# Layer 0 of a two-layer metaformer: where the scan's VectorE instructions wait for the other engines

## The chip, the cores and the metric

The kernel runs on one core of a Trainium2 chip. The metric is the device time of one launch in microseconds (us). A profile is one further execution, recorded by the hardware profiler; its own time stands beside its span below.

## The reference

Two layers, each a token mixer and a small feed-forward network with residuals, over an image of 2 x 96 channels x 96 x 96. Only the mixer of layer 0 is touched. It projects to 192 inner channels, bends the image by a learnt offset, and runs a selective scan over windows of 6 x 6 tokens in four directions (`kg` = 0 to 3), with 16 states for every inner channel:

```python
def step(hst, inputs):
    ut, dt, bt, ct = inputs
    dA = jnp.exp(dt[..., None] * A)
    hst = hst * dA + (dt * ut)[..., None] * bt[:, :, None, :]
    y = jnp.einsum('bkdn,bkn->bkd', hst, ct)
    return (hst, y)
h0 = jnp.zeros((Bt, K_, Dd, N), u.dtype)
_, ys = jax.lax.scan(step, h0, (us, ds, bs, cs))
return jnp.moveaxis(ys, 0, -1) + Dv[None, :, :, None] * u
```

## The kernel before

Layer 0 takes the two images in 32 stripes of 6 image rows (576 tokens, 16 windows). A stripe has three parts: `_l0_front` (norm, projection, convolution, offsets, sampling, the step sizes and B and C of the scan), `_l0_scan` and `_l0_back` (norm, gate, projection, feed-forward).

`_l0_scan` runs, for a stripe, over two halves of the channels (`h`), two token orders (`o`) and two directions (`kk`): eight sections. A section (`_l0_section`) has four quarters (`i`) of four states each, and a quarter has two units (`c` = 0 and 1, 288 tokens each). That is 1024 quarters and 2048 units in all. Counting the units through the whole layer, unit u and unit u+1 with u even make a quarter. Partitions hold 32 channels x 4 states; three channel blocks lie along the free axis, so an operation of a unit has 128 x 864 elements.

A quarter begins with a DMA of C (`cre`) and three ScalarE exponentials (line 997) that make the decays `dA` of both its units, in one of two buffers. A unit is then, in order of the data:

- **B** (line 1008): a TensorE matmul spreads a row of B over the partitions, into one of two PSUM buffers `B`.
- **product** (line 1011): VectorE multiplies it by `dur` (step size times input) into the single PSUM buffer `bp`.
- **scan** (line 1021): VectorE's scan of `dA` and `bp` into one of six buffers `h` (`P.nh` = 6).
- **times C** (line 1024): GpSimd multiplies `h` by `cre` in place.
- **states** (line 1034): TensorE sums over the states into the accumulator `y`.

So a product waits for its B, and for the scan before it, which reads the one buffer `bp`. A scan waits for its product, for its decays, and for the buffer `h` that the unit six before it used: that unit's times C and states. The scan of unit u+1 takes the buffer of unit u-5.

The order on each engine is written out by a planner: `_Plan.op` records every operation with a cost, the tiles that it reads and writes, and a due time; `_Plan.order` plays the engines forward and sorts all operations by planned start; `_Plan.issue` emits them in that order, and `_in_order` holds each engine to it. Semaphore waits are put in afterwards, where an instruction needs a later tick of another engine than its own engine has already waited for.

Of the kernel before, what the change touches and what calls it, by code (L numbers as in the profile page):

```python
# [12 lines left out]
AF = mybir.ActivationFunctionType  # L13
ALU = mybir.AluOpType
# [18 lines left out]
H2 = T // 2  # L33
# [4 lines left out]
NBL = C // CB  # L38
# [17 lines left out]
def _in_order(k, tc, start, engines=ENGINES):  # L56

    last = {}
    for i in k.nc.cur_bb.bb.instructions[start:]:
        if i.engine in engines:  # L60
            if i.engine in last:
                tc.add_manual_dep(
                    i,
                    last[i.engine].name,
                    mybir.DependencyInfo(
                        mybir.DependencyClass.NoSync, mybir.DependencyReason.DATA
                    ),
                    reason="in_order",
                )
            last[i.engine] = i  # L70
# [865 lines left out]
def _l0_scan(k, P, S, n, f, tau):  # L936


    nc = k.nc
    f.Y = S.tile(P.hand, [C, 2, T], "Y", 1)  # L940
    for h in range(2):

        py = S.tile(P.ps, [128, 512], "y", 1)
        t0 = (64 * n + 32 * h) * tau

        def direct(h=h, py=py):

            for b in range(NBL):
                w = k.w_D[:, h, b * CB : b * CB + CB]
                v = f.xs0.ap[:, h]  # L950
                nc.tensor.matmul(py.ap[b * CB : b * CB + CB, :HEAD], w, v[:, :HEAD],
                                 start=True, stop=False)
                nc.tensor.matmul(_tail(py, b), w, v[:, HEAD:], start=b == 0, stop=False)

        S.op("pe", 1.4, direct, (f.xs0,), (py,), due=t0)
        for o in range(2):
            for kk in range(2):
                _l0_section(k, P, S, f, o, h, kk, py, t0 + (16 * o + 8 * kk) * tau, tau)

        def out(h=h, py=py):  # L960
            nc.scalar.copy(f.Y.ap[:, h, :HEAD], py.ap[:C, :HEAD])
            for b in range(NBL):
                nc.scalar.copy(f.Y.ap[b * CB : b * CB + CB, h, HEAD:], _tail(py, b))

        S.op("act", 1.4, out, (py,), (f.Y,), due=t0 + 33 * tau)
# [5 lines left out]
def _tail(py, b):  # L971

    n = T - HEAD
    return py.ap[NBL * CB :, b * n : b * n + n]


def _l0_section(k, P, S, f, o, h, kk, py, at, tau):
    nc = k.nc
    kg = o + 2 * kk
    reps = []  # L980
    for name, d in (("dlr", f.dl[kg]), ("dur", f.du[kg])):
        t = S.tile(P.rep, [128, NBL, T], name, 2)
        S.op("sp", 2.6, lambda t=t, d=d: nc.sync.dma_start(
            t.ap.rearrange("p b t -> p (b t)"),
            d.ap[:, 3 * h : 3 * h + 3, :].rearrange("c b t -> c (b t)").unsqueeze(1)
            .to_broadcast([CB, NQ, NBL * T])), (d,), (t,), due=at - 9 * tau)
        reps.append(t)
    dlr, dur = reps

    def quarter(i):  # L990
        t0 = at + 2 * i * tau
        cre, dA = S.tile(P.rep, [128, T], "cre", 4), S.tile(P.rep, [128, 2, NBL, H2], "dA", P.nda)
        S.op("sp", 1.0, lambda: nc.sync.dma_start(
            cre.ap, f.cd[o].ap[kk, :, i, :].unsqueeze(0).to_broadcast([CB, NQ, T])),
            (f.cd[o],), (cre,), due=t0 - P.early["sp"] * tau)
        for blk in range(NBL):
            S.op("act", 0.76, lambda blk=blk: nc.scalar.activation(  # L997
                dA.ap[:, :, blk, :], dlr.ap[:, blk, :].rearrange("p (c n) -> p c n", c=2),
                AF.Exp, scale=k.A[:, i, kg, h, blk : blk + 1]),
                (dlr,), ((dA, blk),), due=t0 - P.early["act"] * tau, tab="e")  # L1000
        for c in range(2):
            unit(i, c, cre, dA, t0 + c * tau)

    def unit(i, c, cre, dA, t0):
        toks = slice(c * H2, (c + 1) * H2)
        pB, bp = S.tile(P.ps, [128, 512], "B", 2), S.tile(P.ps, [128, 1024], "bp", 1)
        ht = S.tile(P.rep, [128, NBL, H2], "h", P.nh)
        S.op("pe", 0.3, lambda: nc.tensor.matmul(  # L1008
            pB.ap[:, :H2], k.selb[:, kk, i, :], f.bc[o].ap[:, toks], start=True, stop=True),
            (f.bc[o],), (pB,), due=t0 - P.early["pe"] * tau)  # L1010
        S.op("dve", 1.13, lambda: nc.vector.tensor_tensor(  # L1011
            bp.ap[:, : NBL * H2].rearrange("p (b n) -> p b n", b=NBL), dur.ap[:, :, toks],
            pB.ap[:, :H2].unsqueeze(1).to_broadcast([128, NBL, H2]), ALU.mult),
            (dur, pB), (bp,), due=t0 - P.early["dve"] * tau)

        def scan():
            hv, dv = (v.rearrange("p b n -> p (b n)") for v in (ht.ap, dA.ap[:, c]))
            bv = bp.ap[:, : NBL * H2]
            if kk:
                hv, dv, bv = hv[:, ::-1], dv[:, ::-1], bv[:, ::-1]  # L1020
            nc.vector.tensor_tensor_scan(hv, dv, bv, 0.0, ALU.mult, ALU.add)  # L1021

        S.op("dve", 2.0, scan, (dA, bp), (ht,), due=t0 + (1.35 - P.early["dve"]) * tau)
        S.op("pool", 2.06, lambda: nc.gpsimd.tensor_tensor(  # L1024
            ht.ap, ht.ap, cre.ap[:, toks].unsqueeze(1).to_broadcast([128, NBL, H2]), ALU.mult),
            (cre,), (ht,), due=t0 + (2.3 - P.early["pool"]) * tau)

        def states():
            end = o == 1 and kk == 1 and i == NQ - 1

            def part(dst, v, stop):
                if o:
                    v = v.rearrange("p (w j i) -> p w i j", i=WIN, j=WIN)
                nc.tensor.matmul(dst, k.fold, v, start=False, stop=stop)  # L1034

            for blk in range(NBL):
                dst = py.ap[CB * blk : CB * blk + CB]
                n = HEAD - H2 if c else H2
                part(dst[:, c * H2 : c * H2 + n], ht.ap[:, blk, :n], end and c == 1)
            if c:  # L1040
                for blk in range(NBL):
                    part(_tail(py, blk), ht.ap[:, blk, n:], end and blk == NBL - 1)

        S.op("pe", 1.0, states, (ht,), (py,), due=t0 + (3.5 - P.early["pe"]) * tau)

    for i in range(NQ):
        quarter(i)


def _layer0(k, tc, a, x, x2d):  # L1050


    nc = k.nc
    with ExitStack() as st:
        P = Ctx()
        pool = lambda name, bufs, **kw: st.enter_context(tc.tile_pool(name=name, bufs=bufs, **kw))
        cp = pool("l0c", 1)
        P.dram = pool("scr", 1, space=DRAM)
        with ExitStack() as ws:
            tmp = ws.enter_context(tc.tile_pool(name="l0t", bufs=1))  # L1060
            wps = ws.enter_context(tc.tile_pool(name="l0p", bufs=1, space=PSUM))
            _l0_weights(k, a, cp, tmp, wps, P.dram)
            ffn = _ffn_weights(k, cp, tmp, "f0", a["W1_0"], a["b1_0"], a["W2_0"], a["b2_0"])
        P.front, P.hand, P.rep, P.back = (pool(n, 1) for n in ("front", "hand", "rep", "back"))
        P.ps = pool("ps0", 1, space=PSUM)
        P.early = {"pe": 60, "act": 60, "dve": -30, "pool": 0, "sp": 8}
        P.np, P.ng, P.nda, P.nh = 3, 5, 2, 6
        start = len(nc.cur_bb.bb.instructions)
        S, tau = _Plan(k), 3.4
        stripes = [(b, s) for b in range(NB) for s in range(NW)]  # L1070
        F = [Ctx() for _ in stripes]

        def front(n):
            if n < len(stripes):
                t0, t1 = (64 * n - 90) * tau, (64 * n - 12) * tau
                _l0_front(k, P, S, F[n], x, *stripes[n], lambda v: t0 + v * (t1 - t0))

        def back(n):
            b, s = stripes[n]
            t0, t1 = (64 * n + 68) * tau, (64 * n + 135) * tau  # L1080
            _l0_back(k, P, S, F[n], ffn, x[b, :, s * WIN : (s + 1) * WIN, :],
                     x2d[b, :, s * T : (s + 1) * T], lambda v: t0 + v * (t1 - t0))

        front(0)
        for n in range(len(stripes)):
            front(n + 1)
            _l0_scan(k, P, S, n, F[n], tau)
            back(n)
        S.issue()
        _in_order(k, tc, start, ENGINES + (mybir.EngineType.SP,))  # L1090
# [760 lines left out]
```

## Time and profile before

| | us |
|---|---|
| median of 3 runs (9014.46 to 9014.84) | 9014.57 |
| profiled execution, its own time | 9021.88 |
| span of its trace, first to last instruction | 9020.1 |
| first product starts (layer 0's scans begin) | 172.4 |
| last scan starts | 6887.6 |
| VectorE busy in the whole span | 8098.6 (90%) |

Between 172.4 and 6887.6 us the layer's fronts, scans and backs overlap stripe by stripe; what follows is layer 1. In the profile, DVE is VectorE, ACT ScalarE, POOL GpSimd, PE TensorE, PEld TensorE's weight load, and L1021 is line 1021. An instruction of type EVENT_SEMAPHORE carries nothing but waits; the engine's sequencer runs it, and it is not counted as busy. A gap of the engine under 150 ns is not put down to a releaser by the profile: it is shown only in the idle sums.

### The profile page before, as it was taken

Reading aid. Unit: us, or ns where it says so; the run is one execution under the profiler, and the core shown is the slowest. Engines: PE = TensorE matmul, PEld = TensorE weight load, DVE = VectorE, ACT = ScalarE, POOL = GpSimd, SP = SyncE. Lnnn points to the kernel's source line nnn. Section 1 sums busy time; section 2 is a strip of 40 time slices with the busy share of each in tenths; the row PEclk is TensorE's granted clock in tenths of the full one; section 3 lists DMA queues with packets and bytes.
Section 4 is the critical chain, followed back from the end, with each engine's and each line's share of the span. In section 5 each row is a group of like instructions: output and inputs, shape, how many; then the busy total and the mean of one; then the engine's idle time right before and its main releaser. Section 6 shows DMA issues by size and latency. Waiting matters only on the chain.

```text
span 9020.1 us, 122080 instructions
## 1 busy us (share of the span) xinstructions
PE 7473.2 (83%) x43537; PEld 3552.9 (39%) x43537; DVE 8098.6 (90%) x5663; ACT 6393.2 (71%) x10720; POOL 6194.7 (69%) x3931
## 2 busy tenths in 40 slices
PE   6888788888878887888788888878866999989998
PEld 3343334444434443344344444334423333543345
DVE  2999999999999999999999999999996898969988
ACT  4677777777777777777777777777754777677867
POOL 3988888888888888888888888898874000320013
PEclk9889888988888888888898989888866999999999
DMA  2444444444444444444444444444442000010000
GB/s 75 138 140 142 140 139 145 140 141 141 135 140 139 135 147 140 141 142 139 144 140 137 142 136 141 137 140 139 138 140 68 3 3 4 21 30 2 3 9 24
DMA packets 335679, 969.58 MB, mean 107 GB/s; under 512 B 50424, under 2 KB 52144, under 8 KB 334768
## 3 DMA queue, kind: packets, MB, share of 16 engines
q1 hardware_dynamic: 335056, 961.64, 33.7%
q8 instruction: 346, 5.67, 0.3%
q14 instruction: 277, 2.27, 0.1%
HBM read 788.04 MB, written 132.17 MB: 102 GB/s over the span
## 4 chain that ended last, share of the span: by engine, by line
DVE 39%; PE 14%; issue 3%; ACT 2%; POOL 1%; DVEq 1%; DMA 0%; SPq 0%; POOLq 0%; ACTq 0%
DVE h L1021 19%; DVE bp L1011 11%; DVE sums L1426 6%; PE sc L1352 4%; DVE acc L1585 3%; PE av L1413 3%; PE y L1034 1%; PE pp L1601 1%; PE pd L669 0%; PE nxc L1113 0%; POOL e L1550 0%; DVEq L1021 0%; PE pk L1125 0%; PE px L608 0%; PE pv L1157 0%
## 5 line engine op out<-in xcount | busy, mean ns | idle before, releaser
L1024 POOL TENSOR_TENSOR h<-h,cre 128x864 f32<-128x864 f32 x2048 | 4122.8, 2021 | 826.7 <-DVE h L1021 415.0
L1021 DVE TENSOR_TENSOR_SCAN h<-dA,bp 128x864 f32<-128x864 f32 x2048 | 4001.5, 1954 | 252.3 <-PE y L1034 6.4
L997 ACT ACTIVATE dA<-dlr,A 128x576 f32<-128x576 f32 x3072 | 2157.0, 765 | 1219.5 <-DVE h L1021 1127.9
L1011 DVE TENSOR_TENSOR bp<-dur,B 128x864 f32<-128x864 f32 x2048 | 2175.8, 1062 | 257.2 <-DMA dur<-du_d 45.5
L1034 PE MATMUL y<-h,fold 128*32 128x288 f32 (+2 forms) x18432 | 1877.9, 454 | 106.3 <-POOL h L1024 102.2
L1008 PE MATMUL B<-bt,selb 128*128 128x288 bf16 x2048 | 637.6, 313 | 1095.3 <-DVE bp L1011 1087.5
L536 PE MATMUL pc<-xin,off 96*96 96x288 f32 x4608 | 1325.0, 414 | 0.9 <-ACT xin L501 0.9
L1034 PEld LDWEIGHTS y<-h,fold 128*32 128x32 f32 x18432 | 766.0, 119 | 1359.0 <-issue 623.2
L1356 ACT ACTIVATE pr<-sc 128x960 f32<-128x960 f32 (+1 forms) x1080 | 955.4, 937 | 258.0 <-DVE sums L1426 146.1
L1426 DVE TENSOR_TENSOR sums<-sums,pr 128x1920 f32<-128x1920 f32 (+1 forms) x510 | 1059.2, 2077 | 60.2 <-ACT pr L1356 7.0
L536 PEld LDWEIGHTS pc<-xin,off 96*96 96x96 f32 x4608 | 708.0, 164 | 622.8 <-issue 379.9
L1507 POOL MEMSET vch<- 96x32 f32 x16 | 2.0, 125 | 1312.8 <-DVE dist L1385 1269.0
L1352 PE MATMUL sc<-qH,kH 32*128 32x480 f32 (+1 forms) x3240 | 710.2, 602 | 9.8 <-DMA q<-qH 9.8
L1352 PE MATMUL sc<-q,kH 32*128 32x480 f32 (+1 forms) x1080 | 564.3, 602 | 0.0
L1413 PE MATMUL av<-pr,vT 128*32 128x480 f32 (+1 forms) x4320 | 532.9, 564 | 3.8 <-ACT av L1430 3.5
L1585 DVE SCALAR_TENSOR_TENSOR acc<-vch,lepe_w,acc 96x1152 f32<-96x1152 f32 x304 | 489.9, 1612 | 7.6
L1008 PEld LDWEIGHTS <-selb 128*128 128x128 bf16 x2048 | 201.9, 100 | 710.5 <-issue 634.5
L1352 PEld LDWEIGHTS sc<-qH,kH 32*128 32x128 f32 x3240 | 285.0, 184 | 439.6 <-issue 304.3
L709 PE MATMUL pt<-xd,w_dt 96*128 96x288 f32 x768 | 317.5, 506 | 25.9 <-ACT zs L519 13.9
L728 POOL TENSOR_TENSOR e<-e,du 128x576 f32<-128x576 f32 x192 | 271.0, 1412 | 32.2 <-ACT du L724 32.0
L1550 POOL TENSOR_TENSOR e<-e,mask 100x384 f32<-100x384 f32 x96 | 171.5, 1808 | 175.6 <-ACT e L1548 175.3
L730 POOL TENSOR_TENSOR dl<-dl,r 128x576 f32<-128x576 f32 x192 | 270.2, 1407 | 6.2
(260 smaller groups left out, 10182.2 us busy)
## 6 DMA issues: line engine op xcount, KB each, us to landing
cre<-c_d SPq DMA_DIRECT2D x1024, 288.0 KB
dur<-du_d SPq DMA_DIRECT2D x256, 864.0 KB
dlr<-dl_d SPq DMA_DIRECT2D x256, 864.0 KB
x<-xs SPq DMA_DIRECT2D x512, 72.0 KB
du_d<-du SPq DMA_DIRECT2D x128, 288.0 KB
dl_d<-dl SPq DMA_DIRECT2D x128, 288.0 KB
du_d<-du SPq DMA_DIRECT2D x128, 144.0 KB
dl_d<-dl SPq DMA_DIRECT2D x128, 144.0 KB
```

Source lines behind the costliest of these rows:

```text
L536: pe(H2, lambda: nc.tensor.matmul(pc.ap[:C, :H2], k.w_c1[:, ih, tap, oh * C : (oh + 1) * C], xin.ap[:, ih, 3 * c + dy : 3 * c + dy + 3, dx ...
L997: S.op("act", 0.76, lambda blk=blk: nc.scalar.activation(dA.ap[:, :, blk, :], dlr.ap[:, blk, :].rearrange("p (c n) -> p c n", c=2), AF.Exp ...
L1008: S.op("pe", 0.3, lambda: nc.tensor.matmul(pB.ap[:, :H2], k.selb[:, kk, i, :], f.bc[o].ap[:, toks], start=True, stop=True), (f.bc[o],), (p ...
L1011: S.op("dve", 1.13, lambda: nc.vector.tensor_tensor(bp.ap[:, : NBL * H2].rearrange("p (b n) -> p b n", b=NBL), dur.ap[:, :, toks], pB.ap[: ...
L1021: nc.vector.tensor_tensor_scan(hv, dv, bv, 0.0, ALU.mult, ALU.add)
L1024: S.op("pool", 2.06, lambda: nc.gpsimd.tensor_tensor(ht.ap, ht.ap, cre.ap[:, toks].unsqueeze(1).to_broadcast([128, NBL, H2]), ALU.mult), ( ...
L1034: nc.tensor.matmul(dst, k.fold, v, start=False, stop=stop)
L1352: nc.tensor.matmul(two[s // 2][:, s % 2, :n], kH[rows, k0 : k0 + 128], q, start=True, stop=True)
L1356: nc.scalar.activation(pr[:, 2 * i : 2 * i + 2, :n], two[i][:, :, :n], AF.Exp, scale=HD**-0.5)
L1413: nc.tensor.matmul((main if s < HEADS else other)[s * HD : (s + 1) * HD, :n], vT[:, blk, hd, :], pr[:, s, :n], start=at == 0, stop=at == e ...
L1426: nc.vector.tensor_tensor(sums[:, :, :n], sums[:, :, :n], pr[:, :, :n], ALU.add)
L1585: S.op("dve", 1.6, lambda: nc.vector.scalar_tensor_tensor(acc.ap, src(), W.lw[:, t : t + 1], acc.ap, ALU.mult, ALU.add), (vch,), (acc,))
```

## The change

The first product of each quarter (`c` = 0) is given extra dependencies, as semaphore waits: on the last exponential of its quarter, on the B matmul of the unit after it, and on the times C and the last states matmul of unit u-5, whose `h` the quarter's second scan reuses. They are looked up in `P.issued`, a dictionary that is filled as instructions are emitted; what has not been emitted by then is left out. Nothing is said to the other three VectorE instructions of the quarter, which need the same ticks or earlier ones. No operation is added or removed, and costs, tiles and due times given to the planner are the same. `first` is the first unit of the stripe's half, 64 n + 32 h. The last line of the diff stands at the end of `states`.

```diff
-def _l0_section(k, P, S, f, o, h, kk, py, at, tau):
+def _l0_section(k, P, S, f, first, o, h, kk, py, at, tau):
     nc = k.nc
+    latest = lambda: nc.cur_bb.bb.instructions[-1]
+    def wait(keys):
+        for other in map(P.issued.get, keys):
+            if other is not None:
+                P.tc.add_manual_dep(
+                    latest(), other.name,
+                    mybir.DependencyInfo(mybir.DependencyClass.Sync, mybir.DependencyReason.DATA),
+                    reason="with_the_product")
...
-        t0 = at + 2 * i * tau
+        t0, u = at + 2 * i * tau, first + 16 * o + 8 * kk + 2 * i
...
+            def decay(blk=blk):
+                nc.scalar.activation(...)
+                P.issued["act", u] = latest()
...
+        def spread():
+            nc.tensor.matmul(...)
+            P.issued["B", u] = latest()
+
+        def product():
+            nc.vector.tensor_tensor(...)
+            if c == 0:
+                free = u + 1 - P.nh
+                wait([("act", u), ("B", u + 1), ("pool", free), ("pe", free)])
...
+        def times_c():
+            nc.gpsimd.tensor_tensor(...)
+            P.issued["pool", u] = latest()
...
+            P.issued["pe", u] = latest()
```

More of the change, by code (lines that the diff above doesn't have):

```diff
@@ L957, in _l0_scan @@
             for kk in range(2):
-                _l0_section(k, P, S, f, o, h, kk, py, t0 + (16 * o + 8 * kk) * tau, tau)
+                _l0_section(k, P, S, f, 64 * n + 32 * h, o, h, kk, py, t0 + (16 * o + 8 * kk) * tau, tau)
         def out(h=h, py=py):
@@ L996, in quarter, with unit @@
         for blk in range(NBL):
[L997 to L1000, printed above, removed]
+            def decay(blk=blk):
+                nc.scalar.activation(
+                    dA.ap[:, :, blk, :], dlr.ap[:, blk, :].rearrange("p (c n) -> p c n", c=2),
+                    AF.Exp, scale=k.A[:, i, kg, h, blk : blk + 1])
+                P.issued["act", u] = latest()
+            S.op("act", 0.76, decay, (dlr,), ((dA, blk),), due=t0 - P.early["act"] * tau, tab="e")
         for c in range(2):
-            unit(i, c, cre, dA, t0 + c * tau)
-    def unit(i, c, cre, dA, t0):
+            unit(u + c, i, c, cre, dA, t0 + c * tau)
+    def unit(u, i, c, cre, dA, t0):
         toks = slice(c * H2, (c + 1) * H2)
@@ L1007, in unit @@
         ht = S.tile(P.rep, [128, NBL, H2], "h", P.nh)
[L1008 to L1014, printed above, removed]
+        def spread():
+            nc.tensor.matmul(
+                pB.ap[:, :H2], k.selb[:, kk, i, :], f.bc[o].ap[:, toks], start=True, stop=True)
+            P.issued["B", u] = latest()
+        def product():
+            nc.vector.tensor_tensor(
+                bp.ap[:, : NBL * H2].rearrange("p (b n) -> p b n", b=NBL), dur.ap[:, :, toks],
+                pB.ap[:, :H2].unsqueeze(1).to_broadcast([128, NBL, H2]), ALU.mult)
+            if c == 0:
+                free = u + 1 - P.nh
+                wait([("act", u), ("B", u + 1), ("pool", free), ("pe", free)])
+        S.op("pe", 0.3, spread, (f.bc[o],), (pB,), due=t0 - P.early["pe"] * tau)
+        S.op("dve", 1.13, product, (dur, pB), (bp,), due=t0 - P.early["dve"] * tau)
         def scan():
@@ L1023, in unit @@
         S.op("dve", 2.0, scan, (dA, bp), (ht,), due=t0 + (1.35 - P.early["dve"]) * tau)
-        S.op("pool", 2.06, lambda: nc.gpsimd.tensor_tensor(
-            ht.ap, ht.ap, cre.ap[:, toks].unsqueeze(1).to_broadcast([128, NBL, H2]), ALU.mult),
-            (cre,), (ht,), due=t0 + (2.3 - P.early["pool"]) * tau)
+        def times_c():
+            nc.gpsimd.tensor_tensor(
+                ht.ap, ht.ap, cre.ap[:, toks].unsqueeze(1).to_broadcast([128, NBL, H2]), ALU.mult)
+            P.issued["pool", u] = latest()
+        S.op("pool", 2.06, times_c, (cre,), (ht,), due=t0 + (2.3 - P.early["pool"]) * tau)
         def states():
@@ L1065, in _layer0 @@
         P.ps = pool("ps0", 1, space=PSUM)
+        P.tc, P.issued = tc, {}
         P.early = {"pe": 60, "act": 60, "dve": -30, "pool": 0, "sp": 8}
```

## The prediction

> **What bounds the kernel now.** First the page: busy shares, the slices, and the two groups that make the scan.
>
> ```profile
> PE 7473.2 (83%) x43537; PEld 3552.9 (39%) x43537; DVE 8098.6 (90%) x5663; ACT 6393.2 (71%) x10720; POOL 6194.7 (69%) x3931
> ...
> DVE  2999999999999999999999999999996898969988
> ...
> L1021 DVE TENSOR_TENSOR_SCAN h<-dA,bp 128x864 f32<-128x864 f32 x2048 | 4001.5, 1954 | 252.3 <-PE y L1034 6.4
> ...
> L1011 DVE TENSOR_TENSOR bp<-dur,B 128x864 f32<-128x864 f32 x2048 | 2175.8, 1062 | 257.2 <-DMA dur<-du_d 45.5
> ```
>
> VectorE is at 9 in every slice of layer 0, and 6177 us of it are scans and products. Idle time before them sums to 252.3 + 257.2 = 509.5 us. Next, busy time between 150 and 6850 us, and what the idle time before products and scans waited for:
>
> ```profile
> 150.00:6850.00 6700.00, 5375.68 (x31281) 2648.82 (x31284) 6216.28 (x4256) 4790.56 (x8214) 5840.98 (x3612) 0.87 0.44 140
> ```
> ```profile
>   DMA dur<-du_d: 45.5, 1
>   PE B L1008: 12.7, 10
>   PE y L1034: 9.2, 8
>   DVE bp L1011: 5.7, 12
>   ACT dA L997: 5.4, 1
> ```
>
> Columns of the first are PE, PEld, DVE, ACT, POOL: VectorE 93% busy, GpSimd 87%, TensorE 80%, ScalarE 72%. In the second, named waits make only about 82 us, 45.5 of them at the very start. The other 428 us are gaps too short to be named, spread over all 4096 instructions. The waits between engines point the same way: the others wait for VectorE, hardly the reverse.
>
> ```profile
> ACT dA L997 <- DVE h L1021: 1127.9, 611, 4.8
> PE B L1008 <- DVE bp L1011: 1087.5, 1116, 3.0
> POOL h L1024 <- DVE h L1021: 415.0, 368, 2.9
> ```
>
> The gaps are seen in VectorE's timeline (start, duration), and their cause in the instructions of the two lines and of layer 1's `acc` chain:
>
> ```profile
> 3003.10 1.95 DVE L1021 TENSOR_TENSOR_SCAN h<-dA,bp 128x864 f32<-128x864 f32 x1
> 3005.16 1.06 DVE L1011 TENSOR_TENSOR bp<-dur,B 128x864 f32<-128x864 f32 x1
> 3006.36 1.95 DVE L1021 TENSOR_TENSOR_SCAN h<-dA,bp 128x864 f32<-128x864 f32 x1
> 3008.42 1.06 DVE L1011 TENSOR_TENSOR bp<-dur,B 128x864 f32<-128x864 f32 x1
> ...
> 7728.38 2.86 DVE L1585 SCALAR_TENSOR_TENSOR acc<-vch,lepe_w,acc 96x1152 f32<-96x1152 f32 x2
> ```
> ```profile
> L1011 DVEq EVENT_SEMAPHORE  x2034: 21/21/1964, 172.3 to 6886.4; - x185
> L1021 DVEq EVENT_SEMAPHORE  x2082: 21/21/5245, 173.5 to 6887.6; - x190
> L1585 DVEq EVENT_SEMAPHORE  x4: 21/21/21, 7687.7 to 8767.4; - x4
> ```
>
> A product ends at 3006.22 and the scan starts at 3006.36: 0.14 us. Nearly every product and scan has a semaphore instruction ahead of it; 304 `acc` operations have 4 in all, and two in a row take 2.86 us = 2 x 1.415 + 0.03. Sorting VectorE's instructions by the semaphores that they and the instruction ahead of them name gives the gap after the preceding product or scan:
>
> - only VectorE's own semaphore, on the instruction itself: 35 ns (188 `acc` pairs, 16 products and scans);
> - own semaphore on an EVENT_SEMAPHORE, another engine's on the instruction: 103 ns before scans (1032), 104 before products (1653);
> - own and ScalarE's on the EVENT_SEMAPHORE, GpSimd's on the instruction: 132 ns (899 first scans);
> - four engines (PE; VectorE and ScalarE; GpSimd): also 132 ns (37 scans), TensorE's wait being over before the product ends;
> - a DMA's and own: 91 ns (252 first products, once a section).
>
> **What the Trainium skill says.** "Perfetto Trace Analysis", Identifying Dependency Chains: an instruction that waits for several engines may have EventSemaphore instructions put ahead of it. The counts above agree. Same page, Per-engine timelines: a VectorE instruction does its waiting in a queue past the sequencer, a sequencer-only instruction waits in the sequencer. That fits 35 against 103 ns: with its own wait in the sequencer, the operation is passed on only after the wait is over. "VectorE: DVE Perf Modes", The DRAIN you can't avoid, says that a semaphore between operations "costs nothing extra"; this trace differs, and its numbers decide. The same section says that a read after a write on VectorE needs a semaphore: the 35 ns stay.
>
> **The change, part by part.** I count only instructions that directly follow a product or scan; the others (55 first products, 75 second ones, 31 first scans) follow an unrelated operation, overlap it by 80 ns, and gain nothing.
>
> 1. *First scan*: its ScalarE, GpSimd and TensorE ticks have been waited for by its product, so only VectorE is left. 947 fall from 132 to 35, 46 from 103 to 35: 91.9 + 3.1 = 95 us.
> 2. *Second product*: B of unit u+1 has been waited for. 937 follow a scan directly, but in the order that the planner's code and costs give (an order, no time), 65 quarters emit that B after the first product, so the lookup leaves it out. About 877 remain: 877 x 69 ns = 60.5 us.
> 3. *Second scan*: GpSimd of u-5 is covered. 989 x 68 + 32 x 97 ns = 70.4 us.
> 4. *First product*: own, TensorE, ScalarE and GpSimd, the four-engine form. 716 rise from 104 to 132 (20.0 us), 252 with a DMA as well from 91 to 132 (10.3 us). The last form isn't in the trace with five waits. It costs at least 91, as now; at most I take 132 + 50, one more two-wait semaphore instruction of 50 ns after the own one: minus 10 or plus 13 us.
>
> Sum: 225.9 - 30.3 = **195.6 us less**, if no wait is late.
>
> 5. *Late waits*. Behind the waiting product stand its own scan, the second pair, and the unrelated VectorE operations; B of u+2 on TensorE waits for it, and times C, states and the next exponentials for the scans. So all of a stall passes on. From the trace, set against the first product's present start: exponentials end 4.4 us earlier at the median, 2.0 at the 1st percentile; times C of u-5 10.8 and 1.5; states of u-5 7.9 and -2.5; B of u+1 1.8 and -1.7. ScalarE and GpSimd are thus covered. States are late in under 5% of quarters, but there the planner has mostly emitted them after the product: with its order, 2 quarters, 1.0 us. **B of u+1 is the wait that can bite**: it needs the product before (u-1), then TensorE's turn, and is wanted one product and one scan earlier than now. It ends after the product's start in 111 quarters by 56 us; where emitted before it, in 61 quarters (those up to 60 ns early counted in), 20.8 us. Stalls in a row share their lateness, so 20.8 is near the most at today's pace.
> 6. *TensorE's bursts don't shrink.* The chain of waits from 3600 to 6850 us has VectorE lines at 52 + 29%, short pipeline gaps at 5%, TensorE lines at about 9%: B comes just in time there. Over such stretches the gain is lost: 9% of 195.6 = 17 us, some of it the same stalls as in 5. I take 30 us for 5 and 6 together, 10 to 75 as bounds.
>
> No DMA moves: SP's and POOL's queues keep their order. `cre`, `dlr` and `dur` come in at 140 GB/s and 44% of the DMA engines; at a 2.5% higher pace that is 46%. GpSimd goes from 87 to about 90% busy and stays behind VectorE. After layer 0 nothing is changed, so the gain reaches the end in full.
>
> 195.6 - 30 = 166 us. Against the profiled execution, 9021.9 - 166 = 8856; it ran 7.3 us longer than the median 9014.6, so the runs should show about **8849**, rounded to 8850.
>
> **Rivals.**
>
> - *TensorE takes over part of it.* For: the 9%, and 111 late quarters; against: TensorE waits 1087.5 us for products, so it is ahead most of the time. If all 56 us count and as much again comes as VectorE gets faster, 195.6 - 112 = 84: 8931.
> - *Nothing changes.* The waits stay on the later instructions, or the flush between operations takes the gap anyway, as the skill's sentence would have it. Then the gain is the 0 of the scans less part 4's 30 us at worst: 9015, up to 9045. Against: 35 ns after a scan is in this trace, with 13 products and the same data; and first scans already drop their TensorE wait because the product had it.
> - *Slower: every quarter's gate holds VectorE.* Place: the first product, for TensorE's B (or states). It decides once the mean stall passes 195.6 / 1024 = 0.19 us a quarter. At the present mean lateness of 0.34 us that needs 570 quarters, against 61 seen; if 3 in 4 quarters stalled so, 261 us: 9080. It would need TensorE, at 80%, to lose its lead of 1.8 us in the ordinary quarter.
>
> **How the numbers follow.** 0.2% (18 us) is about what a measurement of this kernel can tell from no change. Forecast 0.75, TensorE's part 0.15, nothing 0.05 (of it 0.01 slower), slower 0.05. Faster: 0.75 + 0.15 = 0.90; same 0.04; slower 0.06. The forecast's own range is 195.6 + 10 - 10 at best (8819) to 195.6 - 13 - 75 (8907). Downward the bound on the gaps is that part 4 costs nothing (30 us more, 8789), upward the first rival's 8931. For 8 in 10 I take 8800 to 8930.
>
> **What would show it.** After: hardly any EVENT_SEMAPHOREs left ahead of scans, and some 2100 still on the products' line, two to each first product; idle before scans near 75 us instead of 252; before products 220 to 250 (128 of short gaps before first products, 37 before second ones, 45 at the start, the rest late waits), with PE B as the main named releaser; scan and product durations unchanged at 1954 and 1062; pairs of units in the timeline 6.27 us apart instead of 6.48. It is wrong if gaps before second products stay at 0.10, if DVE bp's named waits for PE pass 100 us, or if states or times C appear there.

## The result, and the profile after

The changed kernel takes 8878.99 us (median of 4 runs, 8876.68 to 8885.70) against 9014.70 before (4 runs): a ratio of 0.9848, 95% interval 0.9834 to 0.9863. That is 135.7 us less (124 to 150 by the interval), where 166 were forecast. The profiled executions differ by 145.2 us of span (9020.1 to 8874.9).

The page of the kernel after: span, slices of VectorE, and the groups of scans (now L1045) and products (now L1030), with the idle time before them behind the second bar.

```profile
span 8874.9 us, 120352 instructions
...
DVE  2999999999999999999999999999996998969988
...
L1045 DVE TENSOR_TENSOR_SCAN h<-dA,bp 128x864 f32<-128x864 f32 x2048 | 3998.7, 1953 | 83.5 <-PE y L1062 5.4
...
L1030 DVE TENSOR_TENSOR bp<-dur,B 128x864 f32<-128x864 f32 x2048 | 2173.8, 1061 | 282.2 <-DMA dur<-du_d 42.3
```

VectorE still bounds layer 0, and its operations take what they took. Idle time before scans fell from 252.3 to 83.5 us; before products it *rose*, from 257.2 to 282.2. The timeline of VectorE (start, duration, and idle time over 150 ns) shows both:

```profile
3006.96 1.95 DVE L1045 TENSOR_TENSOR_SCAN h<-dA,bp 128x864 f32<-128x864 f32 x1
3009.05 1.06 DVE L1030 TENSOR_TENSOR bp<-dur,B 128x864 f32<-128x864 f32 x1
3010.14 1.95 DVE L1045 TENSOR_TENSOR_SCAN h<-dA,bp 128x864 f32<-128x864 f32 x1
3012.13 1.06 DVE L1030 TENSOR_TENSOR bp<-dur,B 128x864 f32<-128x864 f32 x1
3013.23 1.95 DVE L1045 TENSOR_TENSOR_SCAN h<-dA,bp 128x864 f32<-128x864 f32 x1
...
3021.68 1.06 DVE L1030 TENSOR_TENSOR bp<-dur,B 128x864 f32<-128x864 f32 x1 [0.23 <-DVE h L1045]
```

A scan ends at 3008.91 and a first product starts at 3009.05: 0.14. The other three gaps of the quarter are 0.03 to 0.04. Two units are 6.27 us apart (3013.23 - 3006.96), as forecast. The last line is a section's first product, which waits for a DMA as well: 0.23 us.

The semaphore instructions of the two lines:

```profile
L1030 DVEq EVENT_SEMAPHORE  x2057: 21/50/1449, 169.2 to 6734.9; - x187
L1045 DVEq EVENT_SEMAPHORE  x40: 21/21/5271, 170.3 to 6377.8; - x40
```

The scans have lost theirs (2082 to 40); the first products have two each. And the waits named before products and scans (us, times), in part:

```profile
  DMA dur<-du_d: 42.3, 1
  DVE h L1045: 42.0, 174
  PE B L1025: 36.4, 45
  PE y L1062: 11.1, 13
```

"DVE h 42.0, 174" are mostly section-first products with a gap of 0.23 us: VectorE's own semaphore came last, and it is waited for on the first of the two semaphore instructions. TensorE's B went from 12.7 to 36.4 us.

From the first product to the end of the last scan is 6717.2 us before and 6571.9 after, 145.3 less: 140.5 in the gaps between products and scans and 4.8 in the operations themselves. Gaps by position, each counted from the end of the last product or scan, as everywhere below (an unrelated operation in between counts as gap):

| gap before | us before | us after | change | median of direct ones, ns |
|---|---|---|---|---|
| first product | 151.8 | 243.8 | +92.0 | 104 (91 with a DMA) to 133 (231 with a DMA) |
| first scan | 149.5 | 51.5 | -98.0 | 132 to 35 |
| second product | 124.9 | 61.4 | -63.5 | 104 to 34 |
| second scan | 113.6 | 42.7 | -70.9 | 103 to 35 |

For the runs below I use one more number, the **stalls**: over first products with no other operation between them and the scan before, the part over 100 ns of gaps longer than 330 ns. It is 14.2 us before and 52.2 after.

Which wait a stall stood for can be read from TensorE's matmuls, because a product that TensorE has just released starts a fixed time after a matmul's end (the profile models these ends, so it is the regularity that tells). In the kernel before, 8 of the 17 stalled products start 36 to 38 ns after the end of their own B: 11.0 us of the 14.2. In the changed kernel, 51 of 68 start 202 to 205 ns after the end of the B of u+1: 41.6 us of the 52.2. The time is longer because the wait no longer stands on the product, but on the first of two semaphore instructions ahead of it.

### The profile page after: what moved, and what is told of

The parts are those of the page before. It is cut to its first block, busy times and chain, and to the rows that moved or that the text cites. A ratio compares the mean times of both kernels' runs of the same rounds, so it can differ in the third digit from the quotient of the medians.

```text
span 8874.9 us, 120352 instructions
## 1 busy us (share of the span) xinstructions
PE 7426.3 (84%) x43537; PEld 3500.8 (39%) x43537; DVE 8093.4 (91%) x5663; ACT 6381.7 (72%) x10720; POOL 6189.7 (70%) x3931
## 5 line engine op out<-in xcount | busy, mean ns | idle before, releaser
L1045 DVE TENSOR_TENSOR_SCAN h<-dA,bp 128x864 f32<-128x864 f32 x2048 | 3998.7, 1953 | 83.5 <-PE y L1062 5.4
L1030 DVE TENSOR_TENSOR bp<-dur,B 128x864 f32<-128x864 f32 x2048 | 2173.8, 1061 | 282.2 <-DMA dur<-du_d 42.3
L1025 PE MATMUL B<-bt,selb 128*128 128x288 bf16 x2048 | 642.4, 315 | 957.6 <-DVE bp L1030 945.7
```

The source lines that it names most:

```text
L1025: nc.tensor.matmul(pB.ap[:, :H2], k.selb[:, kk, i, :], f.bc[o].ap[:, toks], start=True, stop=True)
L1030: nc.vector.tensor_tensor(bp.ap[:, : NBL * H2].rearrange("p (b n) -> p b n", b=NBL), dur.ap[:, :, toks], pB.ap[:, :H2].unsqueeze(1).to_bro ...
```

## The experiments

Each was timed beside the kernel before, whose median was 9010.1, 9017.9 and 9016.7 us in the three groups (1 to 4, 5 and 6, 7); ratios compare better between groups than times.

**1. Without the wait for the B of unit u+1.**

```diff
-                wait([("act", u), ("B", u + 1), ("pool", free), ("pe", free)])
+                wait([("act", u), ("pool", free), ("pe", free)])
```

> The changed kernel without its wait for the B of unit u+1 at the first product; the other three keys stay. Theory (late B makes VectorE stall at the first product, 45 to 50 us in sum, and would come in time for the second product): the stalls before first products fall from 50 us to under 10, second products go back to the gap of 104 ns from 35 (about 900 x 69 ns = 62 us). Net 12 to 20 us over the changed kernel's 8879: 8890 to 8900. Rival (TensorE's bursts hold VectorE wherever the wait stands): the stalls only move to the second product, 62 us more: about 8940.

8920.33 us, 0.9896 (0.9881 to 0.9911): slower than the changed kernel by 43 us (0.0048 of 9015). Second products went back to 104 ns, 63.5 us, as expected. The stalls fell only from 52.2 to 27.9 us, not below 10:

```profile
  DVE h L1045: 43.8, 181
  PE B L1025: 23.9, 16
  PE y L1062: 12.7, 20
```

The profile names B for 23.9 us. But it names what came last, which need not be what the product waits for. Lines of TensorE and VectorE around one such stall, of unit 1358:

```profile
4564.48 0.42 PE L1025 MATMUL B<-bt,selb 128*128 128x288 bf16 x1
...
4564.95 1.95 DVE L1045 TENSOR_TENSOR_SCAN h<-dA,bp 128x864 f32<-128x864 f32 x1
...
4568.43 0.58 PE L1062 MATMUL y<-h,fold 128*32 128x216 f32 x12
...
4568.95 0.30 PE L1025 MATMUL B<-bt,selb 128*128 128x288 bf16 x1
...
4569.27 1.06 DVE L1030 TENSOR_TENSOR bp<-dur,B 128x864 f32<-128x864 f32 x1 [2.37 <-PE B L1025]
```

The product's own B is the first of these, done at 4564.90. The B that ends 30 ns ahead of the product is that of u+1, for which it doesn't wait here. The last states of u-5 end 258 ns ahead of it. So it is at 9 of the 23 stalled products (238 to 263 ns), 14.5 us of the 27.9. At 7 others the own B ended 203 to 206 ns before: 9.0 us, no more than the kernel before has.

So the expectation held half. The early wait for B costs 24 us (52.2 - 27.9), but half of what is left is another early wait of the change, that for the states of u-5, and a later own B at the faster pace isn't seen. Nor did the stalls move to the second products, as the rival had it; the kernel ended between the two forecasts.

**2. With only the two TensorE keys.**

```diff
-                wait([("act", u), ("B", u + 1), ("pool", free), ("pe", free)])
+                wait([("B", u + 1), ("pe", free)])
```

> The changed kernel with only the two TensorE keys (B of u+1, states of u-5) at the first product; ScalarE and GpSimd are again waited for by the scans. Theory: second products stay at 35 ns (63 us less than before), first products keep the own-and-TensorE form (104 ns, and 91 with a DMA), scans are back at 132 and 103, and late B costs 40 to 50 us. Net 13 to 23 us less than before: 8992 to 9002. Rival (the late waits come from ScalarE or GpSimd, whose releasers the profile also names): B's part costs little and the kernel gains the full 60 us: about 8953.

8977.47 us, 0.9962 (0.9948 to 0.9976): 34 us less than before (22 to 47 by the interval; 46.5 from first product to last scan in the traces), between the two expectations. Second products gained 63.9 us; stalls rose from 14.2 to 32.2, and 28.8 us of them are the B of u+1. The theory had put 40 to 50 us on the early wait; near the old pace it costs 18. The prediction's own count, from the trace of before, was 20.8. The rival fails: the first products don't wait for ScalarE and GpSimd here, and stall for B all the same.

Here the wait for TensorE stands on the product, which starts 36 to 38 ns after a late B, against 202 to 205 in the changed kernel. So 51 x 167 ns = 8.5 us of the changed kernel's 41.6 are not lateness of B, but the longer way from the wait to the product.

**3. The DMA's wait taken off the section's first product**, onto a memset of one element on VectorE just ahead of it. `P.gate` is a tile of 1 x 1, and the DMA of `dur` is noted in `P.issued` like the others.

```diff
         def product():
+            if i == 0 and c == 0:
+                nc.vector.memset(P.gate, 0.0)
+                wait([("dur", u)])
             nc.vector.tensor_tensor(
```

> The changed kernel with a 1 x 1 memset on VectorE ahead of each section's first product, and on it the wait for the DMA of dur; the product keeps the four engines. Theory (231 ns come from a second wait instruction behind the one with the own semaphore): 252 first products fall from 231 to 133 ns, 24.7 us less, the memset lies under the wait: about 8854. Rival (the section's first product is late for another reason, such as the DMA itself, or the memset costs its own duration): no change or up to 40 us more, 8879 to 8919.

8851.36 us, 0.9820 (0.9807 to 0.9834): 25 us less than the changed kernel. The section's first products start at 133 ns where they had 231. They keep their own and ScalarE's wait on one EVENT_SEMAPHORE and GpSimd's on themselves; TensorE's has gone ahead of the memset with the DMA's. In its timeline (section's first product at 3018.43, the scan before it ending at 3018.30):

```profile
3016.35 1.95 DVE L1052 TENSOR_TENSOR_SCAN h<-dA,bp 128x864 f32<-128x864 f32 x1
3018.24 0.06 DVE L1035 MEMSET gate<- 1x1 f32 x1
3018.43 1.06 DVE L1037 TENSOR_TENSOR bp<-dur,B 128x864 f32<-128x864 f32 x1
```

The memset takes 59 ns and starts 58 ns before the scan ends, so it costs nothing. In the changed kernel, with five waits, the own semaphore stands on the first of two EVENT_SEMAPHOREs, and the second follows it before the product. That form costs 98 ns more than the one with four, where the own semaphore stands on the last EVENT_SEMAPHORE; the instruction itself is recorded with 50.

**4. All waits on other engines taken off the products.**

```diff
         def product():
+            nc.vector.memset(P.gate, 0.0)
+            if c == 0:
+                free = u + 1 - P.nh
+                wait([("dur", u), ("B", u), ("act", u), ("pool", free), ("pe", free)])
+            else:
+                wait([("B", u)])
             nc.vector.tensor_tensor(
...
-            if c == 0:
-                free = u + 1 - P.nh
-                wait([("act", u), ("B", u + 1), ("pool", free), ("pe", free)])
```

> All waits on other engines taken off the products: a 1 x 1 memset on VectorE ahead of every product carries them (own B, dur, exponentials, times C and states of u-5 ahead of the first; own B alone ahead of the second), the products and scans wait for VectorE alone. Theory (the gap is long because the own semaphore is waited for in the sequencer; late B is late only for the first product): first products fall from 133 and 231 to 35 ns (70 + 49 us), B's stalls from 50 to about 10 us, 2048 memsets lie inside the 35 ns and the overlap: 150 to 160 us less than the changed kernel, 8720 to 8730. Rival 1 (TensorE has become the bound of the bursts and takes the gain back): 8760 to 8800. Rival 2 (a memset adds its own 60 ns or more to each unit): 8850 to 8900.

8741.08 us, 0.9702 (0.9688 to 0.9715): the fastest version with the whole computation, 3.0% below the kernel before and about 132 us below the changed one (0.0146 of 9015). Its timeline and the instructions of the memset's line:

```profile
3005.24 1.95 DVE L1052 TENSOR_TENSOR_SCAN h<-dA,bp 128x864 f32<-128x864 f32 x1
3007.13 0.06 DVE L1034 MEMSET gate<- 1x1 f32 x1
3007.23 1.06 DVE L1040 TENSOR_TENSOR bp<-dur,B 128x864 f32<-128x864 f32 x1
3008.32 1.95 DVE L1052 TENSOR_TENSOR_SCAN h<-dA,bp 128x864 f32<-128x864 f32 x1
```
```profile
L1034 DVE MEMSET gate<- x2048: 59/59/59, 172.3 to 6593.7; 1x1 f32 x187
L1034 DVEq EVENT_SEMAPHORE  x1275: 21/50/1346, 172.3 to 6588.7; - x183
```

The memset overlaps the scan's end; first and second products start 34 ns after the scan. The same engines are still waited for (the B of u+1 by the second product's memset), and 1275 EVENT_SEMAPHOREs still pass; they no longer stand between VectorE's own semaphore and the operation. Gaps before first products came to 97.8 us (243.8 in the changed kernel), stalls to 19.3. It fell short of the expected 150 us by 18, half of which are stalls that were to fall to 10; neither rival came true.

**5. The same, with the memset ahead of first products alone, which waits for the B of u+1 too.**

```diff
+            if c == 0:
+                free = u + 1 - P.nh
+                nc.vector.memset(P.gate, 0.0)
+                wait([("dur", u), ("B", u), ("act", u), ("B", u + 1), ("pool", free), ("pe", free)])
```

> As in gate_both, but a memset only ahead of the first product of a quarter; it carries the wait for the B of unit u+1 as well, as the changed kernel's product does. Second products have no memset. Theory (the early wait for B of u+1 costs about 20 us, the rest of late B comes from the faster pace): 20 us more than gate_both's 8741: about 8761, with stalls before first products of some 45 us against 21. Rival (the early wait costs nothing of its own at this pace): 8741 or less, since 1024 memsets are saved.

8756.96 us, 0.9709 (0.9695 to 0.9722). This kernel waits for what the changed one waits for; only the instruction that carries the waits is another. So the 125 us that it is below it (0.0139 of 9015) are the clean measure of the form of the waits. Against experiment 4 the traces stand as expected, 43.2 us of stalls against 19.3, and spans of 8751.4 against 8729.8; but the two ratios differ by 6 us only and their intervals overlap, so the runs alone don't part them.

**Which wait was late.** The stalls by the wait that ended last, told from the matmuls' ends as above, in us and in number of first products:

| kernel | own B | B of u+1 | states of u-5 | not assigned |
|---|---|---|---|---|
| before | 11.0, 8 | not waited for | not waited for | 3.2, 9 |
| changed | 0 | 41.6, 51 | 2.6, 2 | 8.0, 15 |
| experiment 1 | 9.0, 7 | not waited for | 14.5, 9 | 4.4, 7 |
| experiment 2 | 0 | 28.8, 42 | 1.3, 2 | 2.2, 6 |
| experiment 4 | 4.8, 5 | not waited for | 11.5, 18 | 3.1, 3 |
| experiment 5 | 0 | 36.4, 45 | 2.7, 2 | 4.1, 3 |

Where the B of u+1 is waited for, it mostly ends after the states and hides their lateness.

**6. Half of the convolution's matmuls left out**, with the planned order kept, in the kernel before, the changed one and the one of 4.

```diff
-            pe(H2, lambda: nc.tensor.matmul(
+            pe(H2, lambda: ih == 0 and nc.tensor.matmul(
...
-                stop=(ih == 1 and tap == 8),
+                stop=(ih == 0 and tap == 8),
```

> The kernel before with half of the 3 x 3 convolution's TensorE matmuls left out (the second half of the input channels, 2304 of 4608 matmuls, some 650 us of TensorE's time); the planned order of all else is the same. Theory (VectorE bounds layer 0 and TensorE's bursts cost it 13 to 15 us): 10 to 20 us less than before, 8990 to 9000. Rival (TensorE holds layer 0 by more than the named waits show): over 40 us less.

> The changed kernel with the same half of the convolution's matmuls left out. Theory (of the 50 us of stalls before first products nearly all are TensorE behind in its bursts, first with work of the front): the stalls fall below 15 us, 35 to 45 us less than the changed kernel's 8879: 8834 to 8844. Rival (the stalls are the price of the early wait as such, whatever TensorE has to do, or come from ScalarE and GpSimd): under 10 us less.

> gate_both with the same half of the convolution's matmuls left out. Theory (of its stalls of 21 us ahead of first products, TensorE's part goes): 10 to 20 us less than gate_both's 8741: 8721 to 8731. Rival (what is left in gate_both is VectorE's own, or ScalarE's): within 5 us of 8741.

9002.71 us, 0.9982 (0.9975 to 0.9989); 8879.43, 0.9842 (0.9828 to 0.9855); 8716.74, 0.9665 (0.9652 to 0.9678).

- *Kernel before*: 15 us less, as expected. In the traces 9 us are a shorter scan phase (stalls 14.2 to 5.3), and the first scan came 21 us sooner, the first front being shorter. VectorE bounds this kernel.
- *Changed kernel*: the expectation missed. No gain, and stalls of 66.7 us instead of 52.2. Most of the late B didn't stand behind the convolution.
- *Kernel of 4*: 33 us less by the ratio, more than expected, but not for the reason given. Stalls rose from 19.3 to 22.7 us and the scan phase from 6424.4 to 6428.4; the first scan came 17 us sooner. The rest isn't explained, and the two profiled executions differ by 8 us only.

Nor are these clean tests, because the granted clock went down with the work:

```profile
core 0: 8882.7 us, clock 0.849
```
```profile
L536 PE MATMUL pc<-xin,off 96*96 96x288 f32 x2304 | 833.9, 494 | 1.5 <-ACT xin L501 1.0
```

The changed kernel ran at 0.893, with a mean of 416 ns for these matmuls. The 494 are a mixture: in both traces the clock switches between full and half, and such a matmul takes 405 ns at full and 687 at half clock. Of those left, 725 of 2304 began at half clock, against 113 of 4608 in the changed kernel.

**What B stands behind.** TensorE's matmuls and VectorE's operations in the timeline around one late B of the changed kernel:

```profile
1649.68 0.40 PE L1025 MATMUL B<-bt,selb 128*128 128x288 bf16 x1 [1.74 <-DVE bp L1030]
1649.87 1.16 PE L608 MATMUL px<-top,ident 96*96 96x288 f32 x2
1650.83 1.16 PE L608 MATMUL px<-bot,ident 96*96 96x288 f32 x2
1651.65 1.06 DVE L1030 TENSOR_TENSOR bp<-dur,B 128x864 f32<-128x864 f32 x1
1651.79 1.16 PE L608 MATMUL px<-top,ident 96*96 96x288 f32 x2
1652.74 1.95 DVE L1045 TENSOR_TENSOR_SCAN h<-dA,bp 128x864 f32<-128x864 f32 x1
1652.75 1.16 PE L608 MATMUL px<-bot,ident 96*96 96x288 f32 x2
1653.85 0.95 PE L1062 MATMUL y<-h,fold 128*32 128x216 f32 x12
1654.73 0.42 PE L1025 MATMUL B<-bt,selb 128*128 128x288 bf16 x1
...
1655.35 1.06 DVE L1030 TENSOR_TENSOR bp<-dur,B 128x864 f32<-128x864 f32 x1 [0.66 <-PE B L1025]
```

The product that frees the buffer ends at 1652.71. TensorE is in the front's `px` matmuls, then does a unit's states, and comes to the next B at 1654.73, which isn't wanted until the second product; the first one waits for it all the same. The places repeat from stripe to stripe: units 12, 14 and 28 of each 64 have 10.0, 5.2 and 12.3 of the 52.2 us.

**7. B sooner in TensorE's written order.** Each B is sorted to just behind the product that frees its buffer and the copies it reads.

```diff
-        return sorted(out, key=lambda o: (o.start, o.no))
+        soon = lambda o: max(p.start for p in o.deps | {o.behind})
+        return sorted(out, key=lambda o: (o.start, 0, o.no) if o.behind is None else (soon(o), 1, o.no))
...
+        b.behind = P.products.get(u - 2)
```

> The changed kernel with each B matmul moved up in TensorE's written order, to just behind the product that frees its buffer and the copies that it reads; all else keeps its order on its engine. Theory (late B stands behind other matmuls that the fixed order puts between two B: px of the front, pd and pp; it is a place in the order, not TensorE's load): the stalls ahead of first products fall from 50 us to 15 to 25, 25 to 35 us less than the changed kernel's 8879: 8844 to 8854. Rival (TensorE now stands idle for products while other work is ready, and states, front and back come later): the stalls stay or grow, 8879 or more.

> gate_both with the same move of the B matmuls in TensorE's order. Theory: its stalls of 18 us fall below 8: 8728 to 8734, against 8741. Rival (as in b_sooner): 8741 or more.

8944.26 us, 0.9918 (0.9904 to 0.9931), and 8814.60, 0.9773 (0.9760 to 0.9787): the rival was right in both. Stalls were 120.8 and 98.4 us, now named for states:

```profile
  PE y L1065: 86.2, 68
  DMA dur<-du_d: 42.1, 1
  ACT xs L618: 27.2, 13
  DVE h L1048: 22.2, 93
```

TensorE waited 1146.8 us for products where it had waited 945.7 in the changed kernel, and the states came late: 94.5 and 84.4 us of these stalls are first products that wait for the last states of u-5, a wait that the change put there. So the late B isn't cured by its place alone while that wait stands at the first product. The same wait has 11.5 of the last 19.3 us of stalls in experiment 4. No kernel that leaves it at the second scan was run, so what that would bring stays open.

## Why the prediction was right, and by how much it was off

- **Bound and mechanism**: right. VectorE's short gaps went, in the size that the kinds of wait had given: 35 for 132, 103 and 104 ns.
- **Parts 1 to 3**: forecast 225.9 us, measured 98.0 + 63.5 + 70.9 = 232.4. Some more second products than counted lost their wait (891, not 877), and first scans after an unrelated operation gained 1.2 us.
- **Part 4, the first term that was off**: four-engine products came out at 133 ns as forecast, but the 252 with a DMA at 231, against 132 taken and 182 as the upper bound. 252 x (231 - 91) = 35.3 us, against 10.3. The step at fault is the bound "one more two-wait semaphore instruction of 50 ns": the recorded 50 ns are not what it adds behind the own wait. Experiment 3 showed 98 ns, and 25 us in the runs.
- **Parts 5 and 6, the second**: 30 us taken, the stalls rose by 38.0. The early wait's 20.8 was good (18.0 in experiment 2). The pace's 17 isn't shown as such: the other 20.0 hold the 8.5 us of the longer way from a late B to the product, a term that the prediction doesn't have, 5.8 us that aren't assigned to a wait, and about 5.6 us of later B and later states. The own B of first products wasn't later at the faster pace (9.0 us in experiment 1, 11.0 before). So that the two parts came near in sum (37.8 without overlap) is in part luck. Part 6 called it TensorE's bursts. That B was late behind other matmuls is shown; that TensorE's load by itself does it is not, as experiment 6 didn't lower it.
- **States**: put at 1.0 us. They cost 2.6 in the changed kernel, but only because B hides them: 14.5 in experiment 1.
- **ScalarE and GpSimd covered**: nearly. By the prediction's own sign, times C was not to appear among the named waits of products; it does, with 7.4 us at 15 products.
- **The rest**: against the profiled execution 145.2 came instead of 166. Parts 1 to 3 brought 6.5 us more, part 4 25 less and parts 5 and 6 8 less; operations that were 4.8 us shorter in sum stood in no part. The median fell by less, 135.7: the profile before ran 7 us above its median, the one after 2 below, and the forecast had let that offset stand. Idle time before products ended at 282 us, above the 220 to 250 forecast, by the same terms.
- **Slips that changed nothing**: 44% at a 2.5% higher pace is 45%, not 46 (the trace after has 0.45); B of u+1 ends after the first product's start in 89 quarters, not 111, the 56 us being right.
- **The Trainium skill**: the "costs nothing extra" of "VectorE: DVE Perf Modes", The DRAIN you can't avoid, was measured on eight copies with a semaphore after each. It doesn't carry over to operations that wait for other engines as well: with nothing but the carrier of the waits changed, experiment 5 took 125 us off the changed kernel. "Perfetto Trace Analysis", Per-engine timelines, fits: a wait in the sequencer comes before the next instruction is fetched (103 ns and more here), one on the operation itself is made in the engine's queue (35 ns).

## What to carry to other kernels

On an engine whose operations depend on each other, look at what stands between the own semaphore and the operation: an own wait alone on the operation cost 35 ns here. Put on an EVENT_SEMAPHORE ahead, with another engine's wait on the operation, it cost 104 alone, 133 together with another engine's (91 with a DMA's), and 231 with one more EVENT_SEMAPHORE behind it. Gathering the waits of several operations on one is a gain if they are all early; a wait that is only wanted later is better left where it is wanted, if the gap there costs less than the stalls. Here the B of u+1 cost 24 us at the first product and saved 64 at the second; the states of u-5 cost 14.5 us in experiment 1 and 11.5 in experiment 4. Before a stall is put down to the releaser that a profile names, see whether the operation waits for it at all. Better still, put waits on other engines on an operation that needs nothing of its own engine: a memset of one element, hidden under the operation before, took them all (132 us in experiment 4).

## What the runs showed of the hardware that was not expected

- A second EVENT_SEMAPHORE behind the one that waits for the own engine added 98 ns, though such an instruction is recorded with 50 (two waits) or 21 (one).
- A 1 x 1 memset on VectorE took 59 ns and began 58 ns before the end of the scan in front of it, on which it didn't depend; with 2048 of them products started 34 ns after the scan, and 35 without (second products of experiment 5).
- A product that a late matmul released started 36 to 38 ns after the matmul's end when the wait stood on the product itself, and 202 to 205 ns after it when the wait stood on the first of two semaphore instructions ahead. With the wait ahead of a memset (experiments 4 and 5) it was 167 to 169 ns.
- Leaving out 2304 of layer 0's matmuls lowered TensorE's granted clock from 0.893 to 0.849 (from 0.886 to 0.843 and from 0.903 to 0.861 in the other two kernels). Of the same group's matmuls, 31% instead of 2% began at half clock, where one takes 687 ns instead of 405. TensorE's busy time between 150 and 6700 us fell from 5322 to 5000 us only.
